# The last chunk's input load in two pieces, and an instruction order from finer leads

## The chip, the cores and the metric

The kernel runs on one core of a Trainium2 chip (trn2). The metric is the device time of one execution in microseconds; the time before is the median of three runs. Beside the times there is one profiled execution with its trace. The engines are TensorE (PE; its weight loads are PEld), VectorE (DVE), ScalarE (ACT), GpSimd (POOL) and SyncE (SP), which here issues nearly all transfers; sixteen DMA engines carry them out.

## The reference

Input `x` is 4 sequences of 1024 steps and 128 channels, in float32. Two layers follow each other, each with a residual and a layer norm.

```python
# layer 1: gated delta rule, 16 heads of 8, a depthwise convolution of 4 taps in front
q = l2norm(silu(conv(silu(x @ Wq.T + bq))))          # k likewise, v without l2norm
a, b = sigmoid(x @ Wa.T + ba), sigmoid(x @ Wb.T + bb)
for t in range(1024):                                # S is 8x8 for each sequence and head
    S = a*S - a*b*outer(S @ k, k) + b*outer(v, k);  o[t] = q @ S
x = layernorm(x + o @ Wo.T + bo)
# layer 2: attention over the 4 sequences at each step, then 8 experts, the best 2 a token
y = ln1(x + attention(x) @ out_w.T + out_b)
p = softmax(y @ gate_w.T + gate_b);  c = the two largest of p, scaled to sum 1
m = sum_e c_e * (relu(y @ w1[e].T + b1[e]) @ w2[e].T + b2[e])
x = layernorm(x + ln2(y + m))
```

## The kernel before, in words

The 1024 steps are cut into 8 chunks of 128 (`T`). Each chunk passes through stages, written as functions of the chunk's number:

- `project(c)` loads the chunk's rows of `x` as `xt` (128 partitions, one a step; 4 sequences by 128 channels in each; L811), transposes them on PE (L816), and makes `z`, the inputs of the convolution, and `gates`. The convolution looks one step ahead, so the load begins one step late, and the last chunk has only 127 rows (`n`). `xt` has one buffer.
- `prepare(c)` convolves (`diag`, L897), sends q, k and v through DRAM (`dr_bounce`) to put heads on partitions, and computes what the recurrence needs: the decays, `kd_r` (k, loaded in two halves at L926 and multiplied by the decay at L1014), and `wt`.
- `recur(c)` runs the recurrence in 16 blocks of 8 steps. Each block is a chain on DVE: product L1095, sum L1101, product L1110, sum L1116, with a small ACT operation at L1086 and L1107. The states and the values go to `su_out` and, at L1139, in one 512 KB store to `dr_su_back`.
- `output(c)` loads these back as `uc` and `sc` (L1157, L1159), and `q_r`, `qg_r` and `k_r`; POOL multiplies (L1173, L1201, L1219), PE sums over heads (L1181, L1205), DVE finishes `o`, which goes through DRAM again.
- `attend(c)` (from L1289 on PE) and `attended(c)` are the output product, the layer norms, the attention over sequences and the gate.
- `experts(group)` scatters the tokens of one or two chunks into rows sorted by expert (indirect transfers of POOL, L1555), runs each tile of 128 rows through its expert's two products (L1596 and L1609 on PE, L1605 on ACT between them), and gathers the results (L1627).

The stages are written down in a staggered order, the next chunks' `project` and `prepare` ahead of `recur` and `output` of the present one, and `experts` between them. The functions are run twice. In the first run `put_in_order` takes every instruction written down, `price` gives it a duration, `connect` finds what depends on what, and `plan` lets `forward` play the five engines' queues, always taking of the ready instructions the one with the lowest rank. Then `Planned` is raised; in the second run the orders found are laid on the five engines, each of which then works strictly in its own order, SP's queue of transfers included.

The rank of an instruction is the (negative) length of what depends on it, plus a lead from the table `LEAD`: one row for each `mark` (each stage of each chunk), one number for every `PIECE` instructions of that stage.

```python
    for k, g in enumerate(groups):
        n = count[g] = count.get(g, -1) + 1
        rank[k] += LEAD[g][n // PIECE]
```

`HOP[v.engine][e]` is the delay in microseconds after which an engine sees that another is done; `OVERLAP` is what two instructions of one engine share. `forward` has TensorE at half speed after idle stretches, and `fillers` puts products of the identity matrix (L612) into the holes that it finds on PE. A transfer is priced by its bytes, whatever its rows (in `price`, and in `forward` where `u.bytes` is set).

Of the kernel before, what the change touches and what calls it, by code (L numbers as in the profile page):

```python
# [51 lines left out]
T = 128  # L52
# [32 lines left out]
class Slots:  # L85
# [32 lines left out]
PE_, DVE_, ACT_, POOL_, SP_ = range(5)  # L118


HOP = (
    (0.0, 0.054, 0.053, 0.054, 0.05, 0.044),
    (0.038, 0.0, 0.033, 0.034, 0.04, 0.03),
    (0.037, 0.035, 0.0, 0.04, 0.04, 0.05),
    (0.09, 0.08, 0.063, 0.0, 0.06, 0.07),
    (0.031, 0.028, 0.026, 0.027, 0.0, 0.017),
)

OVERLAP = (0.0, 0.083, 0.11, 0.043, 0.0)

PIECE = 60
LEAD = (
    (-596, -698,),
    (-695,),
    (1215, 1142,),
    (-239,),
    (-326,),
    (42, 327,),  # L140
    (-717, -154,),
    (-605, -1049,),
    (-810,),
    (-141, -914,),
    (-468,),
    (847, 645,),
    (142, 371,),
    (832, -867,),
    (-1488,),
    (-525, 14,),  # L150
    (21,),
    (154, 573,),
    (-536, 239,),
    (150, -335,),
    (-139, 302, 1084, 833, 618, 867, 306, -62, 535,),
    (-103,),
    (-319, 358,),
    (21,),
    (822, 1113,),
    (325, 133,),  # L160
    (-330, -211,),
    (-341,),
    (-499, -431,),
    (-273,),
    (809, 430,),
    (21, 79,),
    (510, -110,),
    (-99, 422, 15, 260, -43, 347, -211, 876, 125,),
    (-488,),
    (97, -532,),  # L170
    (-438,),
    (334, 1061,),
    (82, -55,),
    (-748, -468,),
    (-347,),
    (-566, -206,),
    (-890,),
    (673, 244,),
    (-525, -84,),
    (-74, -848,),  # L180
    (330, -102, -426, -699, -279, -40, -524, 453, 218,),
    (-566,),
    (129, -1199,),
    (-377, -137,),
    (-533, 514,),
    (378, 91, 339, 237, 165, 545,),
    (172,),
    (-80, 3,),
    (-409, -393, 106, 565, -698, 771,),
)  # L190
WINDOW, DOWN, UP = 3.413, 0.39, 0.77
FILL, FILL_MIN, FILLER = 0.7, 0.5, 0.225
TABLES = {"Silu": 1, "Sigmoid": 2, "Exp": 3}


# [79 lines left out]
def price(u, i, n_in):  # L275
# [58 lines left out]
    u.long = c  # L334
    u.cost = c - OVERLAP[u.engine]

# [80 lines left out]
def forward(units, rank):  # L417


    q = Queue(units, [u.preds for u in units], rank)  # L420
    begin_, end_ = [0.0] * len(units), [0.0] * len(units)
    order = [[] for _ in range(5)]
    size, cols, dma, pool, dve, table = None, [0.0] * 4, 0.0, 0.0, 0.0, 0
    slow, window, busy, carry, holes = True, 0, 0.0, 0.0, []
    for _ in units:
        now, e, k = q.take()
        u = units[k]
        begin = now
        if e == PE_:
            own, col = u.tile  # L430
            if size not in (None, own):
                begin = max(begin, max(cols)) + 0.1
            begin = max(begin, cols[col] if own[1] == 32 else max(cols))
            idle = max(cols + [q.free[e]])
            share = FILL * (begin - idle) if begin - idle > FILL_MIN else 0.0
            if share:
                holes.append((len(order[0]), idle, begin))
            spent = 0.0
            while True:
                t = idle + spent if share else begin  # L440
                while t >= (window + 1) * WINDOW:
                    slow = busy < (UP if slow else DOWN) * WINDOW
                    window, busy, carry = window + 1, carry, 0.0
                if not share:
                    break
                filler = FILLER * (2.0 if slow else 1.0)
                if spent + filler > share:
                    share = 0.0
                else:
                    now_ = min(filler, (window + 1) * WINDOW - t)  # L450
                    busy, carry = busy + now_, carry + filler - now_
                    spent += filler
            cost = u.cost * (2.0 if slow else 1.0)
            if own[1] == 32:
                cols[col] = begin + cost
                q.free[e] = begin + (0.25 if slow else 0.125)
                active = 0.4 * cost
            else:
                cols = [begin + cost] * 4
                q.free[e] = begin + cost  # L460
                active = cost
            now_ = active * max(0.0, min(1.0, ((window + 1) * WINDOW - begin) / cost))
            busy, carry = busy + now_, carry + active - now_
            size = own
            end = begin + cost + u.long - u.cost
        elif u.bytes:
            dma = max(begin + u.cost + 0.2, dma) + u.bytes / 265e3
            end = dma + 1.4
            q.free[e] = begin + u.cost
        else:  # L470
            alone = u.kind in ("TensorTensor", "TensorScalarPtr", "TensorCopy")
            if e == DVE_ and alone and not any(u.psum):
                begin = max(begin, pool)
            if e == POOL_ and alone:
                begin = max(begin, dve)
            if e == ACT_ and u.table and u.table != table:
                begin += 1.28
                table = u.table
            end = begin + u.long
            q.free[e] = begin + u.cost  # L480
            if e == POOL_ and u.kind != "DMACopy":
                pool = end - 0.05
            if e == DVE_ and alone and not any(u.psum):
                dve = end - 0.05
        order[e].append(k)
        begin_[k], end_[k] = begin, end
        transfer = u.kind == "DMACopy"
        for s in u.succs:
            v = units[s]
            if v.engine != e or transfer:  # L490
                q.release(s, end + HOP[v.engine][5 if transfer else e])
            else:
                q.release(s, end if k in v.waits and e != PE_ else begin)
    return begin_, end_, order, holes


def plan(units, groups):


    rank = [0.0] * len(units)  # L500
    for k in range(len(units) - 1, -1, -1):
        u = units[k]
        rank[k] = -u.long + min((rank[s] - 0.05 for s in u.succs), default=0.0)
    count = {}
# [3 lines that stand above are left out]
    begin, end, order, holes = forward(units, rank)  # L508
    return order, max(end), (begin, end, holes)
# [85 lines left out]
def delta_moe_kernel(  # L595
    ctx: ExitStack, tc: tile.TileContext, d: dict, out: bass.AP, planned=None
):
    nc = tc.nc
# [175 lines left out]
    for n in range(2):  # L774
        t = nc.dram_tensor(f"sorted{n}", (NT * P, C), F32).ap()
# [31 lines left out]
    def project(c):  # L807

        xt = pa.tile([P, B, C], F32, tag="xt", name=f"xt{c}", bufs=1)
        n = T if c < NCHUNK - 1 else T - 1  # L810
        nc.sync.dma_start(  # L811
            xt[0:n], d["x"][:, c * T + 1 : c * T + 1 + n, :].rearrange("b t c -> t b c")
        )
        ps = psum.tile([P, B, T], F32, tag="pa", name=f"ps_xT{c}")
        for b in range(B):
            nc.tensor.transpose(ps[:, b, 0:n], xt[0:n, b, :], ident[0:n, 0:n])  # L816
# [837 lines left out]

    mark("project", 0)
    project(0)
    mark("prepare", 0)
    prepare(0)
    mark("weights", 0)
    load_layer_weights()  # L1660
    clear_sorted()
    mark("project", 1)
    project(1)
    mark("prepare", 1)
    prepare(1)
# [7 lines left out]
    attended(0)  # L1673
    mark("project", 2)
    project(2)
    mark("prepare", 2)
    prepare(2)
# [161 lines left out]
```

## Time and profile before

| | |
|---|---|
| times of three runs | 831.64, 833.87, 839.53 us; median 833.87 |
| profiled execution, its own time | 832.78 us |
| its span, first to last instruction | 831.1 us |
| mean granted TensorE clock | 0.953 of full speed |
| PE busy | 699.4 us, 84% |
| DVE busy | 564.6 us, 68% |
| POOL busy | 475.4 us, 57% |
| ACT busy | 412.8 us, 50% |
| moved by DMA | 139.67 MB, 168 GB/s in the mean |

Busy times are sums over the span, in which different engines are loaded at different times. The recurrence, from some 66 to 566 us, keeps DVE busy; the experts, from about 300 us to the end, are PE's and ACT's. A busy PE is not a PE at its peak: its instructions are pipelined, and the fillers count as busy. Granted clock is the share of full speed at which TensorE was let run.

### The profile page before, as it was taken

How to read it: one execution, taken by the hardware profiler on the slowest of the kernel's cores; microseconds unless marked ns; L12 is line 12 of the kernel's file. 1: busy time of each engine (PE TensorE's matmuls, PEld its weight loads, DVE VectorE, ACT ScalarE, POOL GpSimd, SP SyncE). 2: the span in 40 equal slices, each digit the busy share in tenths (PEclk: the TensorE clock that was granted, in tenths of full speed). 3: DMA queues.
4: the chain of work that ended last, by engine and by line, in shares of the span. 5: the costliest groups of instructions: out<-in, count | busy, mean ns of one | idle time of the engine just before them, and what ended most of it. 6: DMA issues, size and time to landing. Idle time of an engine off the chain costs nothing. (4 is left out here: it accounts for less than half of the span.)

```text
span 831.1 us, 15634 instructions
## 1 busy us (share of the span) xinstructions
PE 699.4 (84%) x5000; PEld 516.5 (62%) x5000; DVE 564.6 (68%) x1742; ACT 412.8 (50%) x1163; POOL 475.4 (57%) x656
## 2 busy tenths in 40 slices
PE   8989797889985988999889888799898999977750
PEld 5555545456553673667677577577477878777640
DVE  2167897898977998989899888987426351531303
ACT  5246362555653435486456435455325565465531
POOL 3534339849646748846746987653778621662213
PEclk9999999999997999999989999999899999999995
DMA  7642244252425245378458648568268688788741
GB/s 204 172 136 85 90 128 130 79 178 79 127 89 156 75 148 171 104 218 264 147 175 279 192 124 249 151 193 264 87 203 231 215 231 256 229 243 258 210 124 29
DMA packets 120070, 139.67 MB, mean 168 GB/s; under 512 B 9517, under 2 KB 90933, under 8 KB 119989
## 3 DMA queue, kind: packets, MB, share of 16 engines
q1 hardware_dynamic: 115893, 130.29, 52.0%
q0 software_dynamic: 4096, 8.40, 3.6%
q8 instruction: 39, 0.64, 0.3%
q14 instruction: 42, 0.34, 0.1%
HBM read 99.53 MB, written 39.12 MB: 167 GB/s over the span
## 5 line engine op out<-in xcount | busy, mean ns | idle before, releaser
L1605 ACT ACTIVATE h<-ps_ph,w_e 128x128 f32<-128x128 f32 x396 | 115.0, 368 | 91.2 <-PE ps_ph L1596 46.8
L1609 PE MATMUL ps_pm<-w_e,h 128*128 128x128 f32 x792 | 134.8, 296 | 19.9 <-ACT h L1605 18.6
L1609 PEld LDWEIGHTS ps_pm<-w_e,h 128*128 128x128 f32 x792 | 110.7, 193 | 39.8 <-ACT h L1605 34.9
L1596 PE MATMUL ps_ph<-xlT,w_e 128*128 128x128 f32 x792 | 116.8, 287 | 8.2 <-ACT xlT L1573 4.4
L1596 PEld LDWEIGHTS ps_ph<-xlT,w_e 128*128 128x128 f32 x792 | 101.1, 196 | 21.2 <-ACT xlT L1573 9.3
L897 PE MATMUL ps_pa<-z,diag 128*128 128x512 f32 x192 | 94.3, 620 | 7.8 <-ACT conv L906 3.0
L1627 POOL DMA_INDIRECT yg<-dr_ys,rows_at x64 | 62.2, 972 | 56.1 <-DMA dr_ys<-yl 26.9
L1555 POOL DMA_INDIRECT sorted<-x,rows_at x64 | 63.3, 989 | 49.9 <-DVE rows_at L1551 20.1
L1107 ACT ACTIVATE p<-ps_su,g_block 128x32 f32<-128x32 f32 x127 | 40.3, 317 | 98.4 <-DVE ps_su L1101 95.9
L1201 POOL TENSOR_TENSOR out_work<-sc__0_704,qg_r 128x512 f32<-128x512 f32 x64 | 73.4, 1165 | 14.3 <-PE ps_po L1205 5.7
L1633 DVE SCALAR_TENSOR_TENSOR acc<-yg,g2x,acc 128x128 f32<-128x128 f32 x64 | 24.0, 379 | 72.1 <-DMA yg<-dr_ys,rows_at 71.9
L1110 DVE TENSOR_TENSOR p<-ps_su,kd_r 128x256 f32<-128x256 f32 x127 | 53.1, 418 | 19.2 <-ACT p L1107 18.8
L897 PEld LDWEIGHTS ps_pa<-z,diag 128*128 128x128 f32 x192 | 33.9, 194 | 43.7 <-issue 30.3
L1101 DVE TENSOR_REDUCE ps_su<-z 128x32 f32<-128x288 f32 x128 | 58.1, 454 | 1.9
L1095 DVE TENSOR_TENSOR z<-ps_su,wt 128x256 f32<-128x256 f32 x128 | 53.4, 417 | 8.5 <-ACT su_out L1133 3.9
L1116 DVE TENSOR_REDUCE ps_su<-p 128x32 f32<-128x288 f32 x127 | 57.5, 453 | 1.6
L1173 POOL TENSOR_TENSOR out_work<-uc,q_r 128x192 f32<-128x192 f32 (+3 forms) x64 | 51.0, 827 | 12.3 <-DMA uc<-dr_su_back 11.8
L1219 POOL TENSOR_TENSOR out_work<-k_r,qu 128x128 f32<-128x128 f32 (+6 forms) x64 | 50.7, 818 | 7.8 <-DVE o L1227 5.3
L1086 ACT COPY z<-x 128x32 f32<-128x32 f32 x128 | 30.7, 245 | 38.7 <-DVE ps_su L1101 38.3
L940 POOL TENSOR_TENSOR work<-conv 128x320 f32<-128x320 f32 (+6 forms) x56 | 36.0, 666 | 22.4 <-DVE x L1035 19.5
L1035 DVE TENSOR_REDUCE x<-work 128x128 f32<-128x256 f32 (+6 forms) x56 | 45.5, 812 | 1.2 <-ACT work L1026 0.3
L1252 ACT ACTIVATE acc<-acc,le_nm,le_rs 128x128 f32<-128x128 f32 x64 | 28.1, 496 | 34.0 <-DVE le_nm L1250 34.0
(209 smaller groups left out, 1481.6 us busy)
## 6 DMA issues: line engine op xcount, KB each, us to landing
w_e<-in_wp SPq DMA_DIRECT2D x99, 514.0 KB, 4.7
dr_bounce<-conv SPq DMA_DIRECT2D x24, 256.0 KB, 2.4
xl<-sorted SPq DMA_DIRECT2D x21, 256.0 KB, 3.2
dr_ys<-yl SPq DMA_DIRECT2D x21, 256.0 KB, 5.0
kd_r<-dr_bounce SPq DMA_DIRECT2D x16, 256.0 KB, 3.1
work<-dr_bounce SPq DMA_DIRECT2D x16, 256.0 KB, 4.5
dr_su_back<-su_out SPq DMA_DIRECT2D x8, 512.0 KB
sorted<-yl SPq DMA_DIRECT2D x10, 256.0 KB, 4.3
```

The costliest lines, as they stand in the source:

```text
L897: nc.tensor.matmul(ps, lhsT=diag[:, i, j, :], rhs=z[:, i, :, j : j + T], start=(j == 0), stop=(j == KC - 1),)
L1095: nc.vector.tensor_tensor(z1n[:, :, :, 0:DH], s[:, :, None, :].to_broadcast([P, HD, J, DH]), wt[n // HALF][:, None, here_cut, :].to_broadc ...
L1101: nc.vector.tensor_reduce(u, z1n, AX.X, ADD)
L1110: nc.vector.tensor_tensor(p3[:, :, :, 0:J], u[:, :, None, :].to_broadcast([P, HD, DH, J]), ks[:, None, :, cut].to_broadcast([P, HD, DH, J] ...
L1116: nc.vector.tensor_reduce(ring[:, (n + 1) % (2 * RING), 0 : HD * DH].rearrange("p (d e) -> p d e", e=DH), p3, AX.X, ADD,)
L1173: gp.tensor_tensor(t[:, :, row_of(j) - r0 : row_of(j + 1) - r0], uv[:, :, 0 : j + 1], qv[:, :, j : j + 1].to_broadcast([P, BN, j + 1]), MUL,)
L1201: gp.tensor_tensor(t, sv[:, :, :, d_ : d_ + 1].to_broadcast([P, B, NB, J]), gv, MUL)
L1555: gp.indirect_dma_start(views[(i * 2 + g) * B + s][0 : nt * P, :], bass.IndirectOffsetOnAxis(ap=rows_at[:, g, s : s + 1], axis=0), x2[:, s ...
L1596: nc.tensor.matmul(ps[:, f, :], lhsT=w1[:, f * P : (f + 1) * P], rhs=xlT[:, i, :], start=True, stop=True,)
L1605: nc.scalar.activation(h[:, f, :], ps[:, f, :], AF.Relu, bias=b1[:, f : f + 1])
L1609: nc.tensor.matmul(ps_y[:, i, :], lhsT=h[:, f, :], rhs=w2[:, f, :], start=(f == 0), stop=(f == NF - 1),)
L1627: gp.indirect_dma_start(yg[:, s, :], None, ys[0 : nt * P, :], bass.IndirectOffsetOnAxis(ap=rows_at[:, g, s : s + 1], axis=0),)
```

## The change

There are two changes. First, `project` loads `xt` by two transfers where the number of rows isn't a multiple of 16; this is so for the last chunk alone, whose 127 rows become 112 and 15. Second, the planner is given other numbers: the hop from ACT to PE rises from 0.053 to 0.1 us; a new row `SELF` delays an instruction that needs the result of an earlier one of its own engine (DVE, ACT and POOL); and `LEAD` is a new table with a number for every 30 instructions in place of every 60. Its numbers were searched with durations that were disturbed. `FILL` keeps its value. No arithmetic changes. Lines after the table move down by five.

```diff
 HOP = (
-    (0.0, 0.054, 0.053, 0.054, 0.05, 0.044),
+    (0.0, 0.054, 0.1, 0.054, 0.05, 0.044),
...
+SELF = (0.0, 0.034, 0.031, 0.05, 0.0)
...
-PIECE = 60
+PIECE = 30
 LEAD = (
-    (-596, -698,),
-    (-695,),
-    (1215, 1142,),
+    (-667, -201, -278,),
+    (-988, -529,),
+    (934, 1478, 1218, 1068,),
...
-FILL, FILL_MIN, FILLER = 0.7, 0.5, 0.225
+FILL, FILL_MIN, FILLER = .7, 0.5, 0.225
...
             if v.engine != e or transfer:
                 q.release(s, end + HOP[v.engine][5 if transfer else e])
             else:
-                q.release(s, end if k in v.waits and e != PE_ else begin)
+                q.release(s, end + SELF[e] if k in v.waits and e != PE_ else begin)
...
         n = T if c < NCHUNK - 1 else T - 1
-        nc.sync.dma_start(
-            xt[0:n], d["x"][:, c * T + 1 : c * T + 1 + n, :].rearrange("b t c -> t b c")
-        )
+
+        for lo, hi in ((0, n),) if n % 16 == 0 else ((0, n - n % 16), (n - n % 16, n)):
+            nc.sync.dma_start(
+                xt[lo:hi],
+                d["x"][:, c * T + 1 + lo : c * T + 1 + hi, :].rearrange("b t c -> t b c"),
+            )
```

More of the change, by code (lines that the diff above doesn't have):

```diff
@@ L127 @@
 )
+SELF = (0.0, 0.034, 0.031, 0.05, 0.0)
 OVERLAP = (0.0, 0.083, 0.11, 0.043, 0.0)
-PIECE = 60
+PIECE = 30
 LEAD = (
-    (-596, -698,),
-    (-695,),
-    (1215, 1142,),
[L138 to L189, printed above, removed]
@@ new lines @@
+    (-667, -201, -278,),
+    (-988, -529,),
+    (934, 1478, 1218, 1068,),
+    (-420, -476,),
+    (-702,),
+    (620, 471, 614, 745,),
+    (-290, -153, 84, -307,),
+    (-759, -742, -1280, -1280,),
+    (-1009, -819,),
+    (22, -70, -1051, -803,),
+    (-378,),
+    (1078, 755, 482, 926,),
+    (508, 551, 791, 734,),
+    (1005, 877, -449, -1036,),
+    (-1749, -1664,),
+    (-318, -1095, -84, -4,),
+    (53,),
+    (469, 116, 923, 794,),
+    (-459, -182, 304, 502,),
+    (355, -135, -317, -193,),
@@ new lines @@
+    (-110, -45, 152, 220, 1179, 1196, 729, 790, 968, 1064, 1240, 1309, 570, 372, 265, -12, 879,),
+    (-550, -112,),
+    (-282, -357, 63, 155,),
+    (-402,),
+    (1459, 970, 1448, 1109,),
+    (633, 435, 24, 345,),
+    (-343, -463, -281, -332,),
+    (-1090, -287,),
+    (-1072, -725, -775, -560,),
+    (-101,),
+    (976, 871, 671, 946,),
+    (347, 430, 43, 163,),
+    (716, 392, 110, -171,),
+    (-179, 62, 707, 1072, 162, 214, 631, 663, -17, 173, 94, 583, -183, -139, 1357, 832, 235,),
@@ new lines @@
+    (-830, -764,),
+    (198, 211, -342, -551,),
+    (-904,),
+    (229, 472, 1546, 1152,),
+    (33, -147, -84, 335,),
+    (-793, -548, -1080, -700,),
+    (-562, -313,),
+    (-1098, -791, 169, -431,),
+    (-914,),
+    (848, 1003, 290, 753,),
+    (-321, -346, 4, 364,),
+    (34, 44, -794, -805,),
+    (570, 208, 393, 72, 246, -86, -443, -334, -69, 215, 254, 202, -765, -357, 615, 995, 367,),
+    (-262, -755,),
+    (-366, 259, -1152, -1823,),
+    (-59, -58, -316, -71,),
+    (-775, -905, 547, 378,),
@@ L190 @@
+    (650, 606, -156, 188, 889, 740, 503, 442, 605, 574, 1459,),
+    (590, 363,),
+    (442, 99, -26, -62,),
+    (-327, -159, 37, -95, 320, 151, 591, 832, -481, -467, 812,),
 )
 WINDOW, DOWN, UP = 3.413, 0.39, 0.77
-FILL, FILL_MIN, FILLER = 0.7, 0.5, 0.225
+FILL, FILL_MIN, FILLER = .7, 0.5, 0.225
 TABLES = {"Silu": 1, "Sigmoid": 2, "Exp": 3}
```

## The prediction, made before the changed kernel had run

> **What bounds the kernel now.** I read the page first, for the engines' shares, then a table of the span in stages, then the waits of the one stage that stands out, then the timeline of SyncE (SP, which issues the transfers) inside it. No engine bounds the whole. In the table of stages VectorE is busy 277 of the 306 us from 260 to 566 and TensorE 273 of them; from 566 to 802, when the recurrence is over, TensorE is busy 205 of 236 us; the last 29 us are a chain of gathers and layer norms. The exception is 240 to 260 us: PE busy 9.94, DVE 9.97, ACT 4.88 and POOL 7.89 of 20 us. Microsecond by microsecond (columns: stretch, length, busy us and count on PE, PEld, DVE, ACT, POOL, granted clock, DMA share, GB/s):
>
> ```profile
> 238.00:239.00 1.00, 1.00 (x3) 0.38 (x2) 1.00 (x2) 0.61 (x3) 1.00 (x2) 1.00 0.05 17
> 240.00:241.00 1.00, 1.00 (x4) 0.48 (x3) 1.00 (x3) 0.84 (x2) 1.00 (x4) 1.00 0.07 22
> ...
> 246.00:247.00 1.00, 1.00 (x4) 0.37 (x2) 0.00 (x0) 0.00 (x0) 0.00 (x0) 1.00 0.07 20
> ...
> 249.00:250.00 1.00, 0.00 (x0) 0.00 (x0) 0.00 (x0) 0.00 (x0) 0.00 (x0) 1.00 1.12 349
> ...
> 252.00:253.00 1.00, 0.00 (x0) 0.00 (x0) 0.00 (x0) 0.00 (x0) 0.00 (x0) 0.50 0.13 50
> ```
>
> From 238 to 248 the sixteen DMA engines show a share of 0.07, about one of sixteen, and 20 to 22 GB/s; from 248 to 253 no compute engine does anything. Where the DMA engines were held is in SP's timeline (start, us, line, transfer):
>
> ```profile
> 236.95 0.28 SPq L811 DMA_DIRECT2D xt<-in_x  x1
> 237.33 10.80 SPq L1139 DMA_DIRECT2D dr_su_back<-su_out  x1
> 248.19 0.46 SPq L926 DMA_DIRECT2D kd_r<-dr_bounce  x1
> ```
>
> The load at 236.95 is the last chunk's 127-row `xt`, 254 KB: 254 KB at 22 GB/s is 11.5 us, the length of the trickle. The store issued behind it takes SP 10.80 us, and everything behind that on SP's queue waits. The same line in all eight chunks (duration ns min/median/max) shows this is no property of the store:
>
> ```profile
> L1139 SPq DMA_DIRECT2D dr_su_back<-su_out x8: 327/377/10805, 115.8 to 566.5; - x8
> ```
>
> Who paid is in the waits from 235 to 330 us (total, times, longest):
>
> ```profile
> ACT p L1107 <- DVE ps_su L1101: 16.0, 4, 12.1
> ...
> PE ps_po L1181 <- POOL out_work L1173: 11.2, 2, 9.9
> POOL out_work L1173 <- DMA uc<-dr_su_back: 11.2, 1, 11.2
> DVE kd_r L1014 <- DMA kd_r<-dr_bounce: 9.9, 1, 9.9
> ```
>
> All four engines stop in the same stretch, each behind a transfer or behind an engine that waits for one.
>
> **The split of the load.** Removed: one 127-row transfer. Added: one of 112 rows, one of 15. Without the trickle the store costs SP its median, 0.377 us, so what follows on SP moves up by 10.80 - 0.38 = 10.4 us: kd_r's multiply could start at 253.24 - 10.4 = 242.8, but VectorE is busy until 243.3, so its wait of 9.93 goes in full. POOL's first L1173 could start at 255.74 - 10.4 = 245.3, against 244.5 at its own pace: it keeps 0.8 of 11.2. TensorE's and ScalarE's waits hang on these two. **Worth 9.9 us**, VectorE's being the shortest of what is freed apart from TensorE's 9.86. Does it reach the end? Afterwards VectorE is 91% and TensorE 89% busy to 566, so neither can catch up in idle time, and each engine's order is fixed: what starts 9.9 us earlier everywhere ends so.
>
> What would be late next: the granted clock was 0.50 from 251 to 260 after the stop, and TensorE worked 257.3 to 260 in it. That may return up to 1.5 us; TensorE wasn't the last wait there, so I take 0.
>
> Cost of the split: a second issue on SP, 0.28 to 0.46 us by the eight rows of L811. In the changed order SP issues the store, then the 112 rows, then the second half of kd_r; the 15 rows stand four transfers later. So 112 rows (224 KB) come ahead of kd_r: one issue and, at the 349 GB/s of the row at 249, 0.64 us. VectorE's cover for kd_r was 0.5 us: **+0.6**, between 0 (in the new order another recurrence step stands before kd_r's multiply) and 1.1. The 15 rows are read by transposes that, in the old order, began about 80 us after the load (318 us): they cost nothing, and would cost their landing, some 3 us, only if that cover went.
>
> Here a rule of the Trainium skill speaks against the change. "DMA: Bandwidth & Descriptors", section "Rules for kernel authors", says not to bother with two transfers to disjoint parts of the partitions, since both use all sixteen engines anyway, and that transfers under 64 KB (the 15 rows are 30 KB) are mostly overhead. By the rule the sum is 832.8 + 0.6, no gain. By the row it is 832.8 - 9.9 + 0.6. I follow the row: the rule's reason is that one transfer already spreads over sixteen engines, and a share of 0.07 says this one did not. How the new pieces spread no row shows. The same page, "Why a DMA increments its semaphore by 16 and not by 1", says that the engines used are the largest number up to 16 that divides the outer dimension: 1 for 127, hence 16 for 112 and 15 for 15. If 112 rows spread as the 128-row loads do (landing 2.8 us), the gain stands; if the 15 rows went through one engine, 30 KB at 22 GB/s would hold it 1.4 us.
>
> **The new order.** The hop from ACT to PE (0.053 to 0.1), `SELF`, and 30-instruction leads change only the order in which each engine does the same work. Comparing the built programs: the same instructions but for the split, three activation table loads fewer, and 363 fillers for 343. An instruction stands on average some 3 to 12 places away from its old place on DVE (1744), 3 to 16 on PE (2257 without fillers). The table loads (1.283 us each) are 3.8 us of an engine 50% busy: 0. Twenty fillers are 40 passes, about 0.11 us apart in PE's timeline, 4.4 us; they stand early (36 fewer before place 280 of PE's order, 54 more from there to 1300, 2 more after it), where PE waits for others: 0, or up to 4.4 if the holes are gone.
>
> What can order be worth? From 60 to 566 us VectorE's waits besides kd_r's sum to 43 us: 18.8 (40 times 0.47) for ACT's part of a recurrence step (L1110 behind L1107), inherent when nothing else is ready, and about 25 that order could touch. No row shows the new order, so bounds: half of the 25 gained, -12; or as much lost, +12, four waits of the longest class outside the stop (3.1 us each: DVE L1095 on ACT wt, PE L1337 on DVE prod) uncovered. One thing can be counted: L1101 directly followed by L1110 on DVE, the pair that makes the 0.47 us wait, stands 34 times for 30: +1.9. Against it I take one 3.1 us wait fewer, as leads twice as fine can move a stretch alone: **-1.2**. In the tail the order puts two more tiles of experts(6) after attended(7)'s last matmul (26 for 24 run alone, at gaps of 0.28 to 0.51 us each): under 1 us, in the bounds.
>
> **The sum**, on the profiled execution's own 832.8 (span 831.1): 832.8 - 9.9 + 0.6 - 1.2 = 822.3. It lies 1.1 below the median of the runs shown, 833.9, and inside their spread; I forecast **822 us**.
>
> **Rivals.** A measurement of this kernel can tell about 1% from no change: below 825.5 is faster, above 842.2 slower.
>
> (a) Forecast: the stop goes, order is worth -12 to +2: 811 to 825.5. For it: all engines stop for one transfer. Chance 0.66.
>
> (b) The stop goes, but order gives most of it back, +3 to +12: 826 to 835; centre 829. For it: 34 close pairs for 30, and only 1.6 us of loss is enough to leave (a). Against: the displacements are local.
>
> (c) The load is hidden anyway or its pieces spread no better: another stop follows, 832 to 834. For it: the 112-row form is nowhere in the trace. Against: eight L1139 rows, seven at about 0.38 us, and seven 128-row loads without a stop. With (b) 0.25, of which (c) 0.04.
>
> (d) Slower: a head-of-line wait on PE in the tail. Output(7)'s last matmul and attend(7)'s first are 67 PE places apart in the old order, 55 in the new: 12 matmuls of 0.22 us are 2.6 us less cover for the way of `o` through DRAM, whose slack was about 4 us (issued 642.8, lands in 3.6, used at 650.5). PE's later tiles queue behind it. It decides once the uncovered waits there and in the like place of earlier chunks exceed 9.3 us, and is over 1% slower past 18.7: some six of the 3.1 us class, 832.8 - 9.3 + 19 = 843. Against: the one I can price still has 1.4 us of slack. Chance 0.09.
>
> **Numbers.** Faster 0.66 is (a), same 0.25 is (b) and (c), slower 0.09 is (d). The range is (a) from its gain bound with a little of the clock's return, 809, to (b)'s end, 835.
>
> **What would show it.** Right: no L1139 or other issue on SP above about 1 us beside the last xt, no stretch with DMA share 0.07 and all engines idle, kd_r's 9.9 us wait gone, POOL's L1173 wait under 2 us. The order: DVE's waits on L1107 near 20 us, the time from the end of the recurrence to the end within a few us of 265. Wrong: an issue of 10 us still on SP (c), or the stop gone while waits of PE on ACT, POOL or DVE after 560 grow by more than 9 us (d).

## The result, and the profile after

The change doesn't gain, it loses 0.6%: the median of 20 executions is **840.64 us** (834.47 to 844.77) against 834.13 us (830.74 to 840.11) of the kernel before on the same chip; ratio of after to before 1.0064, 95% interval 1.0043 to 1.0084. The forecast was 822 us, its range ended at 835. The profiled execution took 839.29 us against 832.78: +6.5 us.

The stop that the split was to remove is gone. SP's timeline of the changed kernel around the last chunk's load (start, us, line, transfer; line numbers are five higher below `project`, and the load is at L815):

```profile
238.30 0.32 SPq L1144 DMA_DIRECT2D dr_su_back<-su_out  x1
239.29 0.35 SPq L815 DMA_DIRECT2D xt<-in_x  x1
239.69 0.72 SPq L931 DMA_DIRECT2D kd_r<-dr_bounce  x1
...
243.78 0.44 SPq L815 DMA_DIRECT2D xt<-in_x  x1
```

The store that took 10.80 us takes 0.32, and neither piece of `xt` holds up what follows it. The row of that store over all eight chunks (ns, min/median/max) lost its outlier of 10805:

```profile
L1144 SPq DMA_DIRECT2D dr_su_back<-su_out x8: 320/336/434, 123.1 to 566.3; - x8
```

In the windows of one microsecond (stretch, length, busy us and count on PE, PEld, DVE, ACT, POOL, granted clock, DMA share, GB/s) the sixteen DMA engines are now full, at 399 GB/s, where one of them had trickled at 22, and the engines work where nothing had run:

```profile
240.00:241.00 1.00, 0.86 (x3) 0.43 (x4) 1.00 (x2) 1.00 (x4) 1.00 (x3) 1.00 1.01 399
246.00:247.00 1.00, 1.00 (x5) 0.26 (x4) 0.93 (x3) 0.00 (x0) 1.00 (x3) 1.00 0.89 327
249.00:250.00 1.00, 1.00 (x4) 0.38 (x2) 1.00 (x3) 0.86 (x4) 1.00 (x2) 1.00 0.04 16
```

But the time isn't there. These are VectorE's longest groups of waits from 66 us to the end of the recurrence (us in total, times, longest), first before, then after:

```profile
DVE p L1110 <- ACT p L1107: 18.8, 40, 1.1
DVE kd_r L1014 <- DMA kd_r<-dr_bounce: 9.9, 1, 9.9
DVE prod L1374 <- PE ps_pc L1366: 4.4, 8, 1.6
DVE z L1095 <- ACT su_out L1133: 3.9, 10, 0.7
```

```profile
DVE p L1115 <- ACT p L1112: 26.2, 49, 1.5
DVE z L1100 <- ACT su_out L1138: 5.7, 10, 1.4
DVE prod L1379 <- PE ps_pc L1371: 4.8, 7, 1.5
```

One wait of 9.9 us went. The wait for ScalarE's part of a recurrence step came 49 times instead of 40 and took 7.4 us more in sum, the wait for `su_out` 1.8 us more. Over the whole stretch to the recurrence's end VectorE is idle for 55.5 us against 56.6 before: of the 9.9 us taken out all but 1.1 came back, in small pieces; none of the three groups shown has a wait above 1.5 us. The recurrence ends at 563.9 us against 564.7, so almost nothing of the gain is left there.

Behind it the changed kernel loses. Two rows, before and after, of the table of stages from 560 us on show TensorE with more busy time and a lower clock:

```profile
560.00:840.00 280.00, 211.21 (x1548) 178.56 (x1546) 103.26 (x405) 129.58 (x381) 124.48 (x141) 0.94 0.65 193
```

```profile
560.00:840.00 280.00, 217.12 (x1584) 185.38 (x1582) 100.76 (x399) 130.78 (x386) 125.22 (x141) 0.92 0.66 198
```

From the end of the recurrence to the end are 273.7 us (837.6 - 563.9), before 266.4 (831.1 - 564.7). The last stage itself didn't grow: TensorE's last product lies at 809.2 us, before at 802.5, and 28.4 and 28.6 us follow it. By 570 us TensorE had finished 2888 of its 4314 passes (fillers aside) against 2918 before, although VectorE was even; nearly all of the 30 missing ones are the experts', and at 0.15 and 0.17 us a pass (116.8 and 134.8 us of busy time over 792 passes each, before) they are an estimated 4.5 us. So the change spends its 9.9 us and some 6.5 more, about 16 us in all, and by this estimate some 14.4 of them (9.9 + 4.5) ahead of 570 us.

### The profile page after: what moved, and what is told of

Same layout as the page of the kernel before. It is cut to its first block, busy times and chain, and to the rows that moved or that the text cites. A ratio compares the mean times of both kernels' runs of the same rounds, so it can differ in the third digit from the quotient of the medians.

```text
span 837.6 us, 15722 instructions
## 1 busy us (share of the span) xinstructions
PE 712.1 (85%) x5040; PEld 523.8 (63%) x5040; DVE 562.6 (67%) x1742; ACT 409.8 (49%) x1160; POOL 479.7 (57%) x656
## 5 line engine op out<-in xcount | busy, mean ns | idle before, releaser
L1601 PE MATMUL ps_ph<-xlT,w_e 128*128 128x128 f32 x792 | 120.3, 293 | 16.7 <-ACT xlT L1578 6.7
L1601 PEld LDWEIGHTS ps_ph<-xlT,w_e 128*128 128x128 f32 x792 | 103.4, 200 | 29.5 <-ACT xlT L1578 10.7
L902 PE MATMUL ps_pa<-z,diag 128*128 128x512 f32 x192 | 92.0, 609 | 7.2 <-ACT conv L911 5.0
L1638 DVE SCALAR_TENSOR_TENSOR acc<-yg,g2x,acc 128x128 f32<-128x128 f32 x64 | 27.2, 435 | 81.1 <-DMA yg<-dr_ys,rows_at 80.9
L1115 DVE TENSOR_TENSOR p<-ps_su,kd_r 128x256 f32<-128x256 f32 x127 | 53.2, 419 | 27.0 <-ACT p L1112 26.2
L1224 POOL TENSOR_TENSOR out_work<-k_r,qu 128x320 f32<-128x320 f32 (+7 forms) x64 | 50.7, 819 | 6.0 <-DVE o L1232 3.3
L614 PEld LDWEIGHTS ps_ph<-ident 128*128 128x128 f32 x314 | 41.0, 202 | 7.5 <-issue 7.2
L614 PE MATMUL ps_ph<-ident 128*128 128x128 f32 x314 | 45.2, 290 | 0.0
```

The lines of the kernel that those rows point to most:

```text
L614: nc.tensor.matmul(whole[:, 0:P], lhsT=ident, rhs=ident, start=True, stop=True)
L902: nc.tensor.matmul(ps, lhsT=diag[:, i, j, :], rhs=z[:, i, :, j : j + T], start=(j == 0), stop=(j == KC - 1),)
L1115: nc.vector.tensor_tensor(p3[:, :, :, 0:J], u[:, :, None, :].to_broadcast([P, HD, DH, J]), ks[:, None, :, cut].to_broadcast([P, HD, DH, J] ...
L1601: nc.tensor.matmul(ps[:, f, :], lhsT=w1[:, f * P : (f + 1) * P], rhs=xlT[:, i, :], start=True, stop=True,)
```

## The experiments

They ran on other chips, where the kernel before itself takes 881 to 887 us. Why isn't shown: the changed kernel's trace is 44 us longer there, 5.5 of them ahead of the last store of the recurrence (571.8 us for 566.3), and for a stop of ScalarE of 21.4 us behind it the profile shows nothing that was waited for. So each time is given as a ratio to the kernel before on the same chip. Such ratios still differ between chips: the changed kernel has 1.0064 on the first and 1.0003 on another, and `old_new_experts` has 0.976 and 0.987 on two. Differences below 1% between experiments on different chips say little.

**The two halves of the change, apart.** `split_only` is the kernel before with the new load; its orders are those of before but for one more transfer on SP. `new_unsplit` is the changed kernel with the old load.

```diff
-        nc.sync.dma_start(
-            xt[0:n], d["x"][:, c * T + 1 : c * T + 1 + n, :].rearrange("b t c -> t b c")
-        )
+        for lo, hi in ((0, n),) if n % 16 == 0 else ((0, n - n % 16), (n - n % 16, n)):
+            nc.sync.dma_start(
...
```

> The kernel before with the last load in 112 and 15 rows and nothing else; every engine's order but SP's, which gains the one issue, stays as it was. Theory A (the split's 9.9 us reach the end, and the new order lost some 16): 823 to 825 us, ratio 0.988 to before. Theory B (the stop goes, but its 9.9 us are taken up by a later wait of the same order, as the changed kernel seems to lose them between 454 and 500 us): 831 to 835, ratio 0.997 to 1.002, the recurrence ending near 564 as in both kernels. In both the store's issue on SP is under 0.5 us.

> The changed kernel with the last load again in one transfer of 127 rows: the new order without the split, every other engine's order as in the changed kernel. Theory A (split and order add up): the stop returns and costs 8 to 10 us, 849 to 851, ratio 1.018 to 1.020. Theory B (a stop is made up for later): 840 to 843. Theory C (the new order has the store ahead of the load and so covers the stop): 840 to 842, with the 10 us issue on a transfer behind the load that nobody waits for.

`split_only`: **0.9899** (0.985 to 0.9948). `new_unsplit`: **1.0153** (1.0109 to 1.0196). The forecast's sum holds for the old order: about 9 us of 885, for a wait of 9.9. The new order alone makes the kernel slower: `new_unsplit` and the kernel before share the 127-row load and differ in the order alone, so 1.0153 is the cost of the new order, 1.5%. With one load of 127 rows the stop is there too, but on another instruction, in SP's timeline of `new_unsplit`:

```profile
241.75 0.27 SPq L813 DMA_DIRECT2D xt<-in_x  x1
242.06 11.98 SPq L928 DMA_DIRECT2D kd_r<-dr_bounce  x1
```

It falls on whichever transfer SP issues next.

**What makes the load slow: its number of rows.** Both kernels are `split_only` with another cut.

```diff
-        for lo, hi in ((0, n),) if n % 16 == 0 else ((0, n - n % 16), (n - n % 16, n)):
+        for lo, hi in ((0, n),) if n % 16 == 0 else ((0, 113), (113, n)):   # split_113_14
+        for lo, hi in ((0, n),) if n % 16 == 0 else ((0, 120), (120, n)):   # split_120_7
```

> As split_only, but the two pieces have 113 and 14 rows: as many transfers, the same order. If what held the transfers is the row count that sixteen, or anything up to it, does not divide (113 is prime), the stop returns with 113/127 of its length: an issue of some 9 to 10 us on SP, DMA share 0.07, 832 to 834 us. If any split relieves it, it equals split_only.

> The kernel before with the last load in 120 and 7 rows, the order of split_only on every engine. 15 divides 120 and 7 divides 7, so 15 and 7 DMA engines would carry them. If the piece has only to spread over many engines, it equals split_only: ratio 0.988 to 0.991, no issue over 1 us on SP. If it has to be a multiple of sixteen, the stop returns: ratio 0.998 to 1.001. It also gives the old order with the split a second time, for its trace.

SP's timeline of `split_113_14`, then of `split_120_7`:

```profile
239.03 0.28 SPq L813 DMA_DIRECT2D xt<-in_x  x1
239.40 9.49 SPq L1142 DMA_DIRECT2D dr_su_back<-su_out  x1
248.95 0.46 SPq L929 DMA_DIRECT2D kd_r<-dr_bounce  x1
```

```profile
237.16 0.38 SPq L813 DMA_DIRECT2D xt<-in_x  x1
237.64 0.42 SPq L1142 DMA_DIRECT2D dr_su_back<-su_out  x1
238.11 0.46 SPq L929 DMA_DIRECT2D kd_r<-dr_bounce  x1
```

113 rows stop SP for 9.49 us, which is 113/127 of the 10.80 (9.6); 120 rows, more than 113, don't. The ratios agree, 0.999 (0.996 to 1.0019) and 0.9889 (0.979 to 0.9989), but the second is known so loosely that it is the timeline that settles it. So it is neither the cut in two nor the size of the pieces that helps, but in all four counts tried (127, 113, 120, 112) divisibility: 127 and 113 are prime, 120 is 15 times 8. That is what the Trainium skill says of the outer dimension in "DMA: Bandwidth & Descriptors", section "Why a DMA increments its semaphore by 16 and not by 1". `split_113_14` also shows where the new order loses, since it kept the old order and a stop, and ran on the same chip as `new_unsplit`. The last store of the recurrence (last start in the row) and VectorE's wait for `kd_r`, in `split_113_14`, then in `new_unsplit`:

```profile
L1142 SPq DMA_DIRECT2D dr_su_back<-su_out x8: 4/332/9494, 117.1 to 572.7; - x8
DVE kd_r L1017 <- DMA kd_r<-dr_bounce: 8.6, 1, 8.6
```

```profile
L1141 SPq DMA_DIRECT2D dr_su_back<-su_out x8: 319/332/475, 123.7 to 584.8; - x8
DVE kd_r L1016 <- DMA kd_r<-dr_bounce: 11.8, 1, 11.8
```

The store comes 12.1 us later, of which 3.2 are the longer stop; the spans differ by 10.5 us (879.4 and 889.9). So the new order's loss, here some 9 us, is there when the recurrence ends.

**The planner's two changes, apart.** `old_leads_new_model` is `split_only` with the new `HOP` and `SELF` (417 fillers), `new_leads_old_model` is `split_only` with the new `LEAD` and `PIECE` (408 fillers).

```diff
-    (0.0, 0.054, 0.053, 0.054, 0.05, 0.044),       # old_leads_new_model, and SELF with its use
+    (0.0, 0.054, 0.1, 0.054, 0.05, 0.044),
...
-PIECE = 60                                         # new_leads_old_model, and the new LEAD
+PIECE = 30
```

> split_only with the new hop from ACT to PE and with SELF, but the old leads for 60 instructions: parts the two edits of the planner. It plans 417 fillers for 343. If the new leads are what costs, this is near split_only, within 5 us; if the changed hop and SELF cost, it is slower than the changed kernel or like it, 838 to 846. The leads were not searched with these numbers, so a slower result says less than an equal one.

> The changed kernel with the old hop from ACT to PE and without SELF: the new leads in the old model. It plans 408 fillers for 363. If the new model's numbers cost, it is faster than the changed kernel, 0.990 to 1.004. If leads are only good in the model that they were searched with, it is slower than it, by the filler count 1.015 to 1.023.

1.023 (1.0175 to 1.0285) and 1.029 (1.0203 to 1.0377), both even slower than expected. Each alone is worse than both together, so what the table costs depends on the model beside it. Both tables are poor in a model other than their own.

**Which rows of the table.** `old_new_experts` is `split_only` with every lead of before written twice (`PIECE` 30) and the new rows in the five `experts` stages alone; `old_new_experts_2` is the same once more. `new_then_old_47` is the changed kernel with the old leads, doubled, in its last eight stages, from `attend(6)` on.

```diff
-    (-139, 302, 1084, 833, 618, 867, 306, -62, 535,),      # old_new_experts, the first of five rows
+    (-110, -45, 152, 220, 1179, 1196, 729, 790, 968, 1064, 1240, 1309, 570, 372, 265, -12, 879,),
...
-    (-262, -755,),                                         # new_then_old_47, the first of eight rows
+    (-566, -566,),
```

> split_only with the old model and the old leads, each written twice at 30 instructions, but the five rows of experts from the new table. It plans 336 fillers for 343 and moves nothing before the first experts stage. If the new leads of experts (which put the first tile at place 778 of TensorE's order for 730) are what costs, it is slower than split_only by most of 1.6%: ratio 1.000 to 1.008. If the count of planned fillers, which is the planner's own measure of the holes on TensorE, tells how good an order is (343 gave 0.990, 363 gave 1.006, 417 gave 1.023), it is like split_only or better: 0.984 to 0.992.

> old_new_experts once more (old model, old leads but for the five rows of experts, 336 fillers), for a closer number: it was 0.976 with an interval of 0.965 to 0.987. If that holds, the new leads of experts are a gain of 1% by themselves: 0.973 to 0.985. If it was luck, it equals split_only: 0.986 to 0.993.

> The changed kernel (new model, split) with the old leads for the last eight stages, from attend(6) on; the new leads before. It plans 392 fillers for 363. If the new leads of the tail cost (attended(7) ahead of tiles of experts(6), the place that the prediction's rival (d) named), it is faster than the changed kernel: below 1.006, down to 0.998. If the loss is ahead of the tail, it is no faster, and by the filler count slower: 1.008 to 1.022.

0.9761 (0.9652 to 0.987), in the repeat 0.9866 (0.9811 to 0.9921): not slower than `split_only`, so in the old model the experts' rows do no harm. Old leads in the tail: 1.0152 (1.0079 to 1.0225), slower than the changed table; so putting the old rows back there recovers nothing. That leaves the other rows before `attend(6)`, in keeping with a loss ahead of 570 us; but rows act on each other and on the model, so this elimination is a weak one.

**Fillers.** `new_no_fill` is the changed kernel in the same order with its 363 fillers left out.

```diff
-        if n > 0:
+        if n > 99:
```

> The changed kernel in its own order without a single filler (363 taken out). If fillers take TensorE time that work would have used, it is faster than the changed kernel, ratio 0.997 to 1.004. If they stand in true holes and keep the clock up, it is slower: less clock, 1.01 to 1.04, with more half-speed stretches than the changed kernel's 88 us.

1.0184 (1.0097 to 1.0271). Without fillers it is slower, so the fillers as a whole gain; what the twenty more do by themselves was not tested. Pages of `new_no_fill` and of the changed kernel (`changed_b`, on another chip):

```profile
PE 677.5 (75%) x4314; PEld 468.6 (52%) x4314; DVE 562.6 (62%) x1742; ACT 410.1 (45%) x1160; POOL 478.9 (53%) x656
...
PEclk9888768759889759999899778999997998599695
```

```profile
PE 718.0 (81%) x5040; PEld 529.0 (60%) x5040; DVE 563.8 (64%) x1742; ACT 409.9 (46%) x1160; POOL 479.6 (54%) x656
```

There are 726 passes fewer, and the mean granted clock is 0.845 instead of 0.938: TensorE does less, and yet the kernel takes longer.

**Other searches.** I searched tables of 30-instruction leads by random changes to single leads, keeping what made the planned time shorter, all with the split. `finer_old_2` and `finer_old_3`: old model, durations as they are, from the old leads and from those with the new experts' rows. `old_model_from_new`: old model, from the new table. `new_model_searched`: the new model, from the table of `finer_old_2`. `finer_old_2_b` and `changed_b` are `finer_old_2` and the changed kernel once more, in one session with the last two. First row of each table:

```diff
-    (-596, -698,),
+    (-227, 1700, -2874, -3373,),        # finer_old_2
+    (-1501, -911, -2001, 312,),         # finer_old_3
+    (-270, 848, -985,),                 # old_model_from_new
+    (1311, 1564, -2339, -2473,),        # new_model_searched
```

> split_only with the old model and a lead for every 30 instructions, found by a search from the old leads with undisturbed durations, as the old table at 60 was. It plans 331 fillers for 343. If leads at 30 instructions are what cost (too fine to hold on the chip), it is slower than split_only's 0.990: 0.995 to 1.005. If the count of planned fillers goes with the time, it is faster: 0.975 to 0.988.

> As finer_old_2, searched from the old leads with the new leads of experts in them. It plans 324 fillers. Finer leads cost: 0.995 to 1.005. Fillers tell: the fastest of all, 0.968 to 0.982.

> Split, the old model (hop 0.053, no SELF), and leads at 30 instructions searched with undisturbed durations from the changed kernel's own table. It plans 347 fillers for the changed kernel's 363. If the new table's neighbourhood is what costs, it is like the changed kernel or slower: ratio 1.004 to 1.015. If the new model's numbers (or the disturbed durations of its search) led the order astray, a search in the old model recovers it: 0.975 to 0.995.

> Split, the new model, and leads at 30 instructions searched with undisturbed durations from finer_old_2's table. It plans 408 fillers. If the new model's numbers are what costs, whatever search is made in it, it is at least as slow as the changed kernel: 1.004 to 1.025. If it was the disturbed search, it is faster than the changed kernel: below 1.000.

> finer_old_2 once more, unchanged, since 0.958 was far better than its own expectation. If that holds: 0.953 to 0.963. If part of it belonged to those runs alone: 0.965 to 0.985.

> The changed kernel itself beside the others, so that all ratios have one basis. It was 1.0064 elsewhere. If split and order add up as new_unsplit (1.015) and split_only (0.990) say, it is 1.003 to 1.008 here too.

| kernel | ratio to before | 95% interval | fillers |
|---|---|---|---|
| `finer_old_2` | 0.9576 | 0.9528 to 0.9624 | 331 |
| `finer_old_2_b` | 0.9576 | 0.9521 to 0.9631 | 331 |
| `finer_old_3` | 0.9744 | 0.9695 to 0.9793 | 324 |
| `new_model_searched` | 0.9844 | 0.9771 to 0.9918 | 408 |
| `old_model_from_new` | 0.9872 | 0.9802 to 0.9943 | 347 |
| `changed_b` | 1.0003 | 0.9974 to 1.0033 | 363 |

Every table searched on undisturbed durations beats the changed one. `finer_old_2` beats both kernels by 4% there, so 30-instruction leads aren't at fault. `new_model_searched` lies below 1, so the new model doesn't force a loss; but its search began at the table of `finer_old_2`, which has 0.9576 in the old model, and `old_model_from_new` gains 1.3% on the changed kernel, so the new model may have a part in the loss. The number of fillers that a plan needs had seemed a measure of how good it is, for it rose with the time in nearly every kernel; 408 fillers at 0.9844 end that.

**Disturbed durations.** What remained was the search itself, or one unlucky draw. `disturbed_a` and `disturbed_b` start from the old leads in the old model as `finer_old_2` does, with moves of the same kind, but each table is judged by its mean over four sets of durations, each duration disturbed by 10%. The search made some 2,000 moves in place of 11,000. They differ from each other in the sequence of moves.

```diff
-    (-227, 1700, -2874, -3373,),        # finer_old_2
+    (-595, -585, -887, -2113,),         # disturbed_a
+    (-589, -526, -826, -519,),          # disturbed_b
```

> The split, the old model, and a table of 30-instruction leads searched from the same start as finer_old_2 (the old leads) and with the same kind of moves, but against the mean over four sets of durations, each duration disturbed by a normal factor of 10%. It plans 407 fillers. If disturbing the durations is what spoils a table, it should stand with the changed table and not with the undisturbed searches: 1.00 to 1.04, against 0.958 and 0.974 for the two undisturbed ones from this start. If the disturbance is harmless and the changed table was only an unlucky draw, it should be at or below split_only's 0.990.

> As disturbed_a with other random moves against the same four disturbed sets; 450 fillers planned. Disturbance the cause: 1.00 to 1.05, whatever the draw. Unlucky draw: it falls on the other side of 0.990 from disturbed_a, or both lie below it.

**1.0393** (1.0307 to 1.0479) and **1.0456** (1.0375 to 1.0536): from the same start both are slower than the kernel before and 8 to 9% slower than `finer_old_2`. The stretch of the recurrence tells where, in the table of stages of `finer_old_2_b`, then of `disturbed_b`:

```profile
60.00:560.00 500.00, 441.94 (x3236) 310.60 (x3235) 442.77 (x1300) 264.39 (x755) 329.17 (x452) 0.97 0.51 156
```

```profile
60.00:560.00 500.00, 428.45 (x3023) 301.99 (x3016) 415.46 (x1168) 235.35 (x670) 305.11 (x425) 0.94 0.44 137
```

In the same 500 us VectorE gets through 1168 instructions instead of 1300, ScalarE through 670 instead of 755. The last chunk's store after the recurrence (last start in each row) is issued at 554.5 us there, and at 592.7 us here:

```profile
L1142 SPq DMA_DIRECT2D dr_su_back<-su_out x8: 325/381/538, 115.7 to 554.5; - x8
```

```profile
L1142 SPq DMA_DIRECT2D dr_su_back<-su_out x8: 319/334/450, 120.2 to 592.7; - x8
```

Again it isn't one long wait. The wait for ScalarE's part of a recurrence step, which the change lengthened, is VectorE's largest group in this stretch here too (`finer_old_2_b`, then `disturbed_b`, 66 to 560 us), and grew by only 6 us. Two waits for which the profile knows no releaser (`remote`) add 13.0 us, and whether the order or the chip makes them isn't shown; VectorE's busy time in the rows above differs by 27.3 us:

```profile
DVE p L1113 <- ACT p L1110: 20.0, 37, 2.8
```

```profile
DVE p L1113 <- ACT p L1110: 26.1, 48, 1.4
DVE prod L1377 <- remote: 13.0, 2, 8.9
```

## Why the prediction failed, by its own steps

- **What bounds the kernel: right.** One transfer stopped four engines, and with it the stop went: no long issue on SP, no stretch with all engines idle at a DMA share of 0.07, `kd_r`'s wait gone.
- **Worth 9.9 us, reaching the end unchanged: right in the order it was worked out for.** `split_only` gained 1.0%. In the new order the split gains too: `new_unsplit` has 1.0153, the changed kernel 1.0003 or 1.0064, so 0.9 to 1.5%.
- **The rule against the row: the row was right.** The rule that two transfers to disjoint partitions aren't worth the bother would have left 832.8 + 0.6, no gain; `split_only` measured 0.9899. It fails where the row count leaves the transfer on few engines; the page's other rule, on the divisor, predicted 127 and 113 as slow and 112 and 120 as not.
- **Cost of the split, +0.6: at most that.** The extra issue took 0.44 us, `kd_r`'s issue lies 0.4 us behind the 112 rows, and VectorE has no wait for that transfer left.
- **The new order, -1.2, bounds -12 to +12: this step failed, in sign and size.** On the prediction's own sum the term is 839.3 - 832.8 + 9.9 - 0.6 = about +16 us. Its experiment, with the stop in both kernels, gives 1.5% (1.0153), 13.5 us of 884; with the stop in neither it is 1.0 to 1.7% (1.0003 or 1.0064 against 0.9899). Both ends of the bound were taken from waits present in the trace of before: half of the 25 us that order could touch, or four of its longest waits. The 18.8 us of waits for ScalarE's part of a recurrence step were set aside as inherent, and just this class grew most up to the recurrence's end. The one count made, 34 close pairs for 30, had the right sign: the wait it stands for came 49 times for 40. It was priced at +1.9 and came to +7.4; then a saved wait of 3.1 us, for which no row spoke, turned the sum to -1.2. Two signs named in advance failed with this step: these waits were to stay near 20 us and came to 26.2, and the time behind the recurrence near 265 us came to 273.7.
- **"Against: the displacements are local": not an argument.** A displacement of 3 to 16 places on average was read as small. `disturbed_a` and `finer_old_2` start from the same leads in the same model and end 8% apart.
- **Twenty fillers, 0 to +4.4: not measured apart.** `new_no_fill` shows that all 363 together gain; it doesn't price the last twenty.
- **The rivals.** (b), that order gives most of it back, had the mechanism and a price that ended 4 us short. (d), a wait in the tail, did not happen as described: no long wait of TensorE at the output of the last chunk, an end stage of equal length, and old leads in the tail make it slower, not faster (1.0152). (c) is excluded by the timeline.

**The cause.** Shown: the new order makes the loss (1.0153 with the load as it was), and it is a matter of the table of leads and the model together. With the new model another table has 0.9844, so neither finer pieces nor the new model force a loss; the experts' rows and the tail's rows could not be found guilty, by the weak test above. Shown for a search of my own: judging a table by durations disturbed by 10% ended at a loss of 4 to 5%, in two of two draws, from the start at which undisturbed durations gave a gain of 4%.

The planner itself says much of this ahead of any run. `plan` returns the time at which its last planned instruction ends, a reckoned time, not a measured one. With the old model it is 787.0 us for the old order and 795.1 for the changed kernel's; with the new model 796.4 and 796.5. So even the new model promised nothing of the new order, and the old one a loss of 8 us. For `finer_old_2` it is 778.6, for `disturbed_a` 817.2, for `disturbed_b` 834.3. A search that keeps only what shortens the undisturbed plan can't end above its start at 787.0; so it was the disturbed judge that let these two tables through, not the smaller number of moves, and the measured times follow the plan. The reckoning isn't exact: `old_new_experts` is planned at 793.3 and ran faster than the kernel before.

Likely, not shown: that the changed table came about in the same way, as how its durations were disturbed isn't known. Open: what single instructions make the 16 us, since the waits are many and small, and how much of `finer_old_2`'s 4% there is on the first chip. Beside `changed_b`, on one chip, the last store of the recurrence is issued 17.3 us earlier in `finer_old_2_b` (554.5 against 571.8), and it ends 40.6 us earlier (spans 841.1 and 881.7), so more than half of its gain lies behind the recurrence, where those chips lose most of their time.

## What to carry to other kernels

Where a change removes a stop and re-plans the order as well, the stop can be read off the trace and the order can't: give the order a term of its own, as wide as several per cent, and measure the removal of the stop with the order held still. Compare the planner's own end times of the two orders, under one model, before anything else: here they differed by 8 us the wrong way. That instructions moved by only a few places says nothing on the sum. And look at the row count of every transfer on a busy queue: one odd last chunk can hold all engines for ten microseconds, and a cut at a row count with a large divisor up to 16 frees them.

## What the runs showed of the hardware that was not expected

An issue on SP that stands behind the load of 127 or 113 rows is held for some ten microseconds, whichever transfer it is: 10.80 us for the store, 11.98 us for `kd_r`, 9.49 us behind 113 rows, against 0.3 to 0.5 us otherwise. And matrix products that compute nothing pay: without the 363 fillers (726 passes) the granted clock was 0.845 instead of 0.938, and the ratio 1.0184 instead of 1.0003 or 1.0064.
